# Depthwise taps moved from VectorE to ScalarE and accumulating transfers in one more unit per image

## Chip, cores and metric

The kernel runs on one core of one Trainium2 chip. The metric is the device time of one execution in microseconds (us), the median of several runs. Five engines of the core work side by side, each through its own instructions in a fixed order: TensorE (PE, matrix products), VectorE (DVE), ScalarE (ACT), GpSimd (POOL, here the issuer of accumulating transfers) and SyncE (SP, the issuer of the other transfers). An instruction that needs a result of another engine waits for it, and what stands behind it in the same queue waits too.

## What is computed

The input is 32 images of 96 channels and 56x56 points in fp32. Layer 0 is an inverted bottleneck with a residual. Layer 1 works on the 3136 points of an image as tokens: a frequency mixer and a small feed-forward part with rounded operands, each behind a layer norm and with a residual. Cut to what matters:

```python
h = relu(bn(einsum('oc,bchw->bohw', w1, x)))    # 96 -> 576 channels
h = relu(bn(dwconv3x3(h, wdw)))                 # nine taps for each channel
x = x + bn(einsum('oc,bchw->bohw', w2, h))      # 576 -> 96 channels
t = tokens(x)
t = t + attn(ln(t))     # 96 -> 192, DFT over tokens, scale, relu, inverse DFT, 192 -> 96
t = t + ffn(ln(t))      # 96 -> 384 -> 96 with fp8 products
```

The change concerns the depthwise convolution alone: each of 576 channels is multiplied by nine weights at nine offsets, and the nine products are summed.

## The kernel before

**Units.** An image is cut in two halves of 28 rows (s = 0 and 1). The hidden channels 0 to 511 are four blocks of 128 (k = 0 to 3); one half of one block is a *unit* (`unit`, line 595), eight per image, 256 in all. The last 64 channels go another way: `last_channels` runs their taps on TensorE as products with banded matrices (lines 719 to 784).

**A unit.** TensorE expands 96 channels to 128 (L617) into PSUM, and ScalarE evicts two pieces with bias and relu into the tile `hs` of 29 rows (L627). ScalarE then starts the sum `acc` with one tap and the bias (L643, `begin`). The other taps reach `acc` in one of two ways. As a rule VectorE does a tap as one multiply-add over the whole tile (L670, `tap`). The tap (0,0) always goes the second way: ScalarE writes weight times `hs` into a tile `product` (L659), and a transfer that adds on arrival, issued by GpSimd, adds that tile to `acc` (L678, `add`). In blocks k = 1 and 3 (`DOUBLE`, line 143) a second tap, (-up, 0), is also a ScalarE product; a first transfer adds it to the product of tap (0,0), and a second adds the sum to `acc`. So a unit with one product has seven taps on VectorE and one transfer, and a unit with two has six taps and two transfers. At the end ScalarE applies relu to `acc` in place (L687, `finish`). Here up = 1 - 2s, so that in the second half (-up, 0) is the tap (1, 0), which covers 27 of the 28 rows.

**The rest of an image.** `front` multiplies the finished units with w2 and the residual's identity in PSUM (L883, L902, L920), and ScalarE evicts (L933); a layer norm on VectorE follows. `mixer_in`, `mid` and `back` are products on TensorE with evictions on ScalarE and some VectorE work in between (among them L987 to L1042, L1123 to L1263, L1329 to L1463).

**Buffers.** `hs` has 3 buffers, `acc` 7, `product` 3; PSUM has 3 general tiles (`ps`) and one for `front` (`pw`).

**What sets the order.** No scheduler of the compiler does; the kernel holds a planner (`Plan`). Each piece of work is a step with an engine, an assumed cost, the steps that it waits for, the buffers that it takes and frees, an assumed delay until others see its result, and a rank. The planner walks through time, and whenever an engine is free it emits there the ready step of lowest rank whose buffers are free. The order that comes out is the fixed order of each engine's instructions on the chip. Every image advances the rank by 32 and every unit by 4; `OFF` and `AT` place the parts of a unit around that (product of tap (0,0) at +3.0, second product at +0.5).

**Fillers.** Where the planner finds TensorE idle with work left[...], it puts in a dummy 128x128 product (`filler`, L1491)[...]. A filler is part of the fixed order: on the chip it runs at its place whether TensorE would be idle or not. One filler shows as two records in the profile.

Of the kernel before, what the change touches and what calls it, by code (L numbers as in the profile page):

```python
# [142 lines left out]
DOUBLE = (1, 3)  # L143
# [15 lines left out]
class Plan:  # L159
# [54 lines left out]
    def step(self, engine, cost, emit, after=(), take=(), give=(), late=None, rank=None):  # L214
        late = self.LATE.get(engine, 0.1) if late is None else late
        if rank is None:
            rank = self.now
            self.now += self.pace
        s = Step(engine, cost, emit, list(after), list(take), list(give), late, rank, len(self.steps))
        self.steps.append(s)  # L220
        return s
# [62 lines left out]
def tile_kernel(ctx: ExitStack, tc: tile.TileContext, d: dict, out: bass.AP):  # L284
# [12 lines left out]
    def psum():  # L297
        return psa.tile([128, 2, 512], F32, name="ps", tag="ps")
# [131 lines left out]
    def scale_of(g, v, p, n):  # L430
        s, r, w = tmp(p, n), tmp(p, n), tmp(p, n)
        nc.vector.tensor_scalar_add(v, v, EPS)
        nc.scalar.activation(r, v, AF.Sqrt)
        newton(s, r, v, w)
        nc.vector.tensor_mul(s, s, g)
        return s
# [6 lines left out]
    s = scale_of(vec[:, 0, :], vec[:, 3, :], 128, NK + 1)  # L443
# [14 lines left out]
    s = scale_of(vec[:, 4, :], vec[:, 7, :], 128, NK + 1)  # L458
# [97 lines left out]
    def pe(n, m, passes):  # L556
        return passes * max(0.855 * n, 0.88 * m) / 1000

    def act(n, columns=0, source=0.05):
        return source + 0.835 * n / 1000 + 0.093 * columns  # L560

    def dve(n, fixed=0.13):
        return fixed + n / 960
# [36 lines left out]
    def unit(img, s, k):  # L600
        n = (2 * img + s) * NK + k
        o = R * s - base[s]
        up = 1 - 2 * s
        u = {}

        def weight(dr, dc):
            at = 3 * (dr + 1) + dc + 1
            return wdw[:, k, at : at + 1]

        def expand(h):  # L610
            def mm():
                if h == 0:
                    u["hs"] = w2.tile([128, XR, S], F32, name="hs", bufs=3)
                u[h] = psum()
                for j in range(2):
                    at = (2 * h + j) * QW
                    nc.tensor.matmul(  # L617
                        u[h][:, j, 0:QW],
                        lhsT=w1T[:, 128 * k : 128 * (k + 1)],
                        rhs=xs[img, s][0:C, at : at + QW],  # L620
                        start=True,
                        stop=True,
                    )

            def evict():
                flat = u["hs"].rearrange("p r c -> p (r c)")
                nc.scalar.activation(  # L627
                    flat[:, 2 * h * QW : 2 * (h + 1) * QW].rearrange("p (j w) -> p j w", j=2),
                    u[h][:, :, 0:QW],
                    AF.Relu,  # L630
                    bias=b1[:, k : k + 1],
                )

            after = [loaded[img, s]] if h == 0 else [u["first"]]
            e = u["first"] = step("PE", pe(QW, 128, 4), mm, after, ["ps"] + ["hs"] * (h == 0), rank=4 * n + OFF[0] + h)
            return step("ACT", act(2 * QW, 1), evict, [e], [], ["ps"], rank=4 * n + OFF[0] + h)

        e = [expand(0), expand(1)]

        def begin():  # L640

            acc[img, s, k] = w1.tile([128, R, S], F32, name="acc", bufs=7)
            nc.scalar.activation(  # L643
                acc[img, s, k],
                u["hs"][:, o + up : o + up + R, :],
                AF.Identity,
                scale=weight(up, 0),
                bias=bd[:, k : k + 1],
            )

        def span(dr, dc):

            return max(0, -(o + dr)), min(R, XR - o - dr), max(0, -dc), S - max(0, dc)

        def product(dr):
            def f():
                ra, rb, _, _ = span(dr, 0)
                u["p", dr] = w1.tile([128, R, S], F32, name="product", bufs=3)
                nc.scalar.activation(  # L659
                    u["p", dr][:, ra:rb, :], u["hs"][:, ra + o + dr : rb + o + dr, :], AF.Copy, scale=weight(dr, 0)  # L660
                )

            return f

        def tap(dr, dc):
            def f():
                ra, rb, ca, cb = span(dr, dc)
                src = u["hs"][:, ra + o + dr : rb + o + dr, ca + dc : cb + dc]
                dst = acc[img, s, k][:, ra:rb, ca:cb]
                nc.vector.scalar_tensor_tensor(dst, src, weight(dr, dc), dst, ALU.mult, ALU.add)  # L670

            return f

        def add(to, dr):
            def f():
                ra, rb, _, _ = span(dr, 0)
                t = acc[img, s, k] if to is None else u["p", to]
                nc.gpsimd.dma_start(  # L678
                    out=t[:, ra:rb, :].rearrange("p r c -> p (r c)"),
                    in_=u["p", dr][:, ra:rb, :].rearrange("p r c -> p (r c)"),  # L680
                    accum_op=ALU.add,
                )

            return f

        def finish():
            nc.scalar.activation(acc[img, s, k], acc[img, s, k], AF.Relu)  # L687

        t = step("ACT", act(W, 2, 0.09), begin, e, ["acc"], rank=4 * n + OFF[1])
        c = [step("ACT", act(W, 1, 0.09), product(0), e, ["product"], rank=4 * n + AT[0])]  # L690
        rest = [q for q in TAPS[1:] if q != (up, 0)]
        if k in DOUBLE:

            rest.remove((-up, 0))
            c.append(step("ACT", act(W, 1, 0.09), product(-up), e, ["product"], rank=4 * n + AT[1]))
        for at, q in enumerate(rest):
            last = q == rest[-1]
            t = step("DVE", dve(W - 28, 0.16), tap(*q), [t] + c * last, [], ["hs"] * last, rank=4 * n + OFF[2] + at * 3.5 / len(rest))
        if k in DOUBLE:
            c = [step("POOL", 1.0, add(0, -up), c, [], ["product"], late=(W * 128 * 4, SOFT), rank=4 * n + AT[1])]  # L700
        t = step("POOL", 1.0, add(None, 0), [t] + c, [], ["product"], late=(W * 128 * 4, SOFT), rank=4 * n + 3)
        ready[img, s, k] = step("ACT", act(W, 0, 0.09), finish, [t], rank=4 * n + OFF[3])
# [775 lines left out]
    for i in range(nimg):  # L1478
        for s in range(2):
            load_half(i, s)  # L1480
            last_channels(i, s)
            for k in range(NK):
                unit(i, s, k)
            front(i, s)
        for half in range(2):
            mid(i, half)
        for h in range(4):
            back(i, h)
# [70 lines left out]
```

## Time and profile before

The median of three runs is 4476.41 us (4473.82 to 4477.92). The profiled execution has a span of 4469.5 us.

| engine | busy, us | share of the span | instructions |
|---|---|---|---|
| PE | 4366.5 | 98% | 34916 |
| DVE | 4307.1 | 96% | 7053 |
| ACT | 4103.5 | 92% | 5390 |
| POOL | 339.6 | 8% | 403 |

The granted TensorE clock is 0.994 of full speed on average. The 16 DMA engines move 789.43 MB; the queue of the accumulating transfers (q0, software_dynamic) has 304.64 MB of it and takes 34.2% of the engines' time.

How to read it: a share of busy time is taken over the whole span, with its start (filling the pipeline) and its end (emptying it). In the long middle part the same pattern repeats: the first `acc` transfers of successive images start 134.6 us apart from the fifth image on. What one image costs there, times the images, makes up most of the time. In the view of groups of instructions each row gives a line of the kernel, the engine, the operation, the tiles, the shape, the count, the busy time in all, the mean of one in ns, and the idle time of the engine just before them with what ended it. Durations of neighbours overlap a little on ACT, DVE and PE[...].

### The profile page before, as it was taken

The page shows a single profiled execution, that of the slowest core. Times are in us where ns is not written, and L with a number is a line of the kernel's source. Part 1 is how long each engine was busy: PE and PEld are TensorE (multiplying, and loading weights), DVE is VectorE, ACT ScalarE, POOL GpSimd, SP SyncE. Part 2 cuts the span into 40 slices and gives each one's busy share as a digit, 9 for nine tenths or more (in the row PEclk, how much of TensorE's full clock was granted, in tenths as well). Part 3 has the DMA queues.
Part 4 walks back from the last instruction along what each step waited for, and adds up shares of the span by engine and source line. Part 5 has one row for each costly group of instructions (what it writes and reads, how often), then busy time and mean ns, then how long its engine had stood idle before and what let it go on. Part 6 is the DMA issues. An engine that isn't in the chain of part 4 may idle for free.

```text
span 4469.5 us, 87997 instructions
## 1 busy us (share of the span) xinstructions
PE 4366.5 (98%) x34916; PEld 3248.3 (73%) x34916; DVE 4307.1 (96%) x7053; ACT 4103.5 (92%) x5390; POOL 339.6 (8%) x403
## 2 busy tenths in 40 slices
PE   8999999999999999999999999999999999999998
PEld 5767777777777777777777777777777777777777
DVE  8999999999999999999999999999999999999977
ACT  5778999999999999999999999999999999999975
POOL 1100000000000000000000000000000000000000
PEclk9999999999999999999999999999999999999999
DMA  5667777777777777777777777777777777777763
GB/s 106 144 147 174 192 172 184 189 176 183 192 171 188 187 176 184 189 176 184 187 173 191 187 174 188 182 176 192 184 176 188 176 180 194 180 177 191 169 180 107
DMA packets 390992, 789.43 MB, mean 177 GB/s; under 512 B 135696, under 2 KB 236628, under 8 KB 390580
## 3 DMA queue, kind: packets, MB, share of 16 engines
q1 hardware_dynamic: 335028, 479.15, 38.1%
q0 software_dynamic: 55488, 304.64, 34.2%
q8 instruction: 275, 4.51, 0.4%
q14 instruction: 137, 1.12, 0.1%
q10 hardware_dynamic: 64, 0.01, 0.0%
HBM read 286.38 MB, written 192.68 MB: 107 GB/s over the span
## 4 chain that ended last, share of the span: by engine, by line
PE 37%; DVE 32%; ACT 15%; issue 3%; DMA 3%; ACTq 0%; DVEq 0%; POOLq 0%; SPq 0%
DVE acc L670 20%; PE pw L883 10%; PE ps L617 5%; PE ps L1005 3%; PE ps L1036 3%; PE ps L1123 3%; PE ps L1329 2%; ACT h L1395 2%; DVE sb L1152 2%; DVE V L1152 2%; DMA acc<-product 2%; ACT product L659 1%; ACT hs L627 1%; PE ps L755 1%; PE ps L1447 1%
## 5 line engine op out<-in xcount | busy, mean ns | idle before, releaser
L670 DVE SCALAR_TENSOR_TENSOR acc<-hs,wdw,acc 128x1540 f32<-128x1540 f32 (+2 forms) x1664 | 2970.5, 1795 | 5.9 <-ACT acc L643 0.3
L617 PE MATMUL ps<-xs,w1T 96*128 96x406 f32 x2048 | 808.9, 517 | 27.2 <-ACT al L784 12.9
L883 PE MATMUL pw<-w2T,acc 128*112 128x96 f32 x7168 | 788.6, 264 | 3.8 <-ACT acc L687 3.7
L883 PEld LDWEIGHTS pw<-w2T,acc 128*112 128x112 f32 x7168 | 750.5, 179 | 57.5 <-issue 34.6
L659 ACT ACTIVATE product<-hs,wdw 128x1568 f32<-128x1568 f32 (+1 forms) x384 | 610.8, 1599 | 15.2 <-DMA product<-product 15.0
L617 PEld LDWEIGHTS ps<-xs,w1T 96*128 96x128 f32 x2048 | 355.6, 190 | 291.5 <-issue 165.1
L627 ACT ACTIVATE hs<-ps,b 128x812 f32<-128x812 f32 x512 | 481.3, 940 | 84.4 <-PE ps L617 79.5
L678 POOL DMA_DIRECT2D acc<-product x256 | 223.3, 872 | 3709.6 <-DVE df L855 687.2
L643 ACT ACTIVATE acc<-hs,bd,wdw 128x1568 f32<-128x1568 f32 x256 | 436.9, 1707 | 0.2
L755 PE MATMUL ps<-hl,band 128*64 128x385 f32 (+3 forms) x3072 | 418.7, 497 | 4.8 <-ACT hs L627 4.8
L687 ACT ACTIVATE acc<-acc 128x1568 f32<-128x1568 f32 x256 | 388.0, 1516 | 26.1 <-DMA acc<-product 19.9
L1005 PEld LDWEIGHTS ps<-watt,xnT 97*120 97x120 f32 x1792 | 293.2, 182 | 97.3 <-issue 40.8
L1005 PE MATMUL ps<-watt,xnT 97*120 97x192 f32 x1792 | 339.1, 330 | 19.8 <-DVE V L1152 14.7
L1123 PEld LDWEIGHTS ps<-wb,yb 112*128 112x128 f32 x3528 | 297.0, 164 | 48.1 <-issue 35.8
L1410 ACT ACTIVATE h<-h 128x784 fp8e5<-128x784 f16 x348 | 300.2, 863 | 34.4 <-DVE h L1401 34.3
L1395 ACT ACTIVATE h<-ps 128x784 f16<-128x784 f32 x384 | 317.0, 828 | 12.3 <-PE ps L1383 11.5
L1350 ACT ACTIVATE u<-tt,mf,rf 112x96 fp8e5<-112x96 f32 x812 | 317.0, 465 | 0.7
L1123 PE MATMUL ps<-wb,yb 112*128 112x112 f32 x3528 | 317.2, 269 | 0.0
L755 PEld LDWEIGHTS ps<-hl,band 128*64 128x64 f32 (+1 forms) x3072 | 152.7, 135 | 203.0 <-issue 163.4
L1401 DVE TENSOR_SCALAR h<-h,b1q 128x784 f16<-128x784 f16 x384 | 162.3, 423 | 88.9 <-ACT h L1395 88.8
L1036 PE MATMUL ps<-z,wa 56*64 56x384 f32 (+1 forms) x2048 | 223.9, 498 | 1.7 <-ACT hs L627 1.7
L1329 PE MATMUL ps<-gd,wd 114*112 114x96 f32 x1792 | 200.2, 264 | 2.3 <-DMA gd<-gdr 2.0
(171 smaller groups left out, 6621.3 us busy)
## 6 DMA issues: line engine op xcount, KB each, us to landing
acc<-product POOLq DMA_DIRECT2D x256, 784.0 KB, 8.7
product<-product POOLq DMA_DIRECT2D x128, 756.0 KB, 11.2
yb<-ydr SPq DMA_DIRECT2D x252, 294.0 KB
wd<-in_wd_dram SPq DMA_DIRECT2D x128, 349.1 KB
wb<-in_wb_dram SPq DMA_DIRECT2D x63, 686.0 KB
ydr<-ya SPq DMA_DIRECT2D x256, 168.0 KB
xs<-in_x_dram SPq DMA_DIRECT2D x64, 609.0 KB
tdr<-xt SPq DMA_DIRECT2D x64, 588.0 KB
```

The source lines that it names most:

```text
L617: nc.tensor.matmul(u[h][:, j, 0:QW], lhsT=w1T[:, 128 * k : 128 * (k + 1)], rhs=xs[img, s][0:C, at : at + QW], start=True, stop=True,)
L627: nc.scalar.activation(flat[:, 2 * h * QW : 2 * (h + 1) * QW].rearrange("p (j w) -> p j w", j=2), u[h][:, :, 0:QW], AF.Relu, bias=b1[:, k ...
L643: nc.scalar.activation(acc[img, s, k], u["hs"][:, o + up : o + up + R, :], AF.Identity, scale=weight(up, 0), bias=bd[:, k : k + 1],)
L659: nc.scalar.activation(u["p", dr][:, ra:rb, :], u["hs"][:, ra + o + dr : rb + o + dr, :], AF.Copy, scale=weight(dr, 0))
L670: nc.vector.scalar_tensor_tensor(dst, src, weight(dr, dc), dst, ALU.mult, ALU.add)
L687: nc.scalar.activation(acc[img, s, k], acc[img, s, k], AF.Relu)
L755: nc.tensor.matmul(pv[:, :, ca:cb], lhsT=band[rows, j, dc + 1, 64 * o : 64 * o + 64], rhs=H[rows, q : q + 7, ca + dc : cb + dc], skip_grou ...
L883: nc.tensor.matmul(u["pw"][0:SK, t, n % 4, 0:C], lhsT=src[rows, (G * t + n) * SK : (G * t + n + 1) * SK], rhs=rhs, skip_group_check=True, **k,
L1005: nc.tensor.matmul(pv[0:PK, q - a, 0:HA], lhsT=xnT[:, q, 0:PK], rhs=watt, start=True, stop=True,)
L1036: nc.tensor.matmul(u["y", b][64 * c : 64 * c + n, j, 0 : 2 * HA], lhsT=wa[at, 0:n], rhs=rhs, start=True, stop=True)
L1123: nc.tensor.matmul(o, lhsT=lhsT, rhs=u["wb"][:, G * s + q, :], start=True, stop=True)
L1395: nc.scalar.activation(u["h", c].rearrange("p (j w) -> p j w", j=2), u["H", c][:, :, 0:n], AF.Copy)
```

## The change

One more unit per image, the first block of the second half (k = 0, s = 1), sends two taps through ScalarE and the accumulating transfers. It is meant to take work off VectorE and give it to ScalarE, whose share of busy time is lower, and to the transfers. Nothing else is edited; ranks, buffers and the planner's constants stay. Since all orders come from the planner, the orders of all engines are made anew.

```diff
         rest = [q for q in TAPS[1:] if q != (up, 0)]
-        if k in DOUBLE:
+        double = k in DOUBLE or (k == 0 and s == 1)
+        if double:
 
             rest.remove((-up, 0))
             c.append(step("ACT", act(W, 1, 0.09), product(-up), e, ["product"], rank=4 * n + AT[1]))
         for at, q in enumerate(rest):
             last = q == rest[-1]
             t = step("DVE", dve(W - 28, 0.16), tap(*q), [t] + c * last, [], ["hs"] * last, rank=4 * n + OFF[2] + at * 3.5 / len(rest))
-        if k in DOUBLE:
+        if double:
             c = [step("POOL", 1.0, add(0, -up), c, [], ["product"], late=(W * 128 * 4, SOFT), rank=4 * n + AT[1])]
         t = step("POOL", 1.0, add(None, 0), [t] + c, [], ["product"], late=(W * 128 * 4, SOFT), rank=4 * n + 3)
```

## The prediction

> **What bounds the kernel now.** I read the busy time in stretches first, since start and end differ from the middle: 0 to 400 us fills the pipeline, 800 to 4000 us repeats one image, the rest empties it. The columns are stretch, length, then busy us and instructions of PE, PEld, DVE, ACT and POOL, the TensorE clock, the DMA share and GB/s.
>
> ```profile
> 0.00:400.00 400.00, 363.03 (x2628) 264.36 (x2628) 366.15 (x431) 273.42 (x282) 39.25 (x58) 0.96 0.64 142
> ...
> 800.00:4000.00 3200.00, 3164.86 (x25406) 2337.00 (x25408) 3143.53 (x5093) 3076.81 (x4089) 247.17 (x285) 1.00 0.75 183
> 4000.00:4470.00 470.00, 447.67 (x3755) 353.47 (x3751) 406.38 (x898) 375.16 (x520) 21.94 (x25) 0.99 0.63 161
> ```
>
> In the middle PE is busy 98.9%, DVE 98.2%, ACT 96.1%. An image takes 134.6 us there (from one image's first `acc` transfer to the next one's), so per image PE is idle 1.5 us, DVE 2.4, ACT 5.2. Only in the first 400 us is ACT far below DVE (273 against 366).
>
> Three engines so near to full need a second look: who waits for whom. These are the waits of 800 to 4000 us, first of DVE, then ACT, then PE (total us, times, longest).
>
> ```profile
> DVE h L1401 <- ACT h L1395: 50.7, 71, 1.2
> ```
>
> ```profile
> ACT al L784 <- PE ps L755: 43.8, 47, 1.0
> ACT hs L627 <- PE ps L617: 39.1, 49, 1.2
> ACT h L1410 <- DVE h L1401: 29.9, 46, 0.9
> ACT acc L687 <- DMA acc<-product: 0.3, 1, 0.3
> ```
>
> ```profile
> PE ps L1005 <- DVE V L1152: 11.2, 23, 0.5
> PE ps L617 <- ACT al L784: 10.8, 47, 0.2
> PE ps L617 <- ACT h L1395: 7.7, 25, 0.4
> ```
>
> DVE waits almost only for ACT (2.1 us per image: 50.7 x 134.6/3200), never for an `acc`, a `product` or a lack of taps. ACT waits mostly for PE (82.9 us of its waits, 3.5 per image). PE waits little for anybody (29.7 us, 1.25 per image). The lag starts at PE and travels to ACT and then to DVE. The chain of waits of one image (2053 to 2188 us) says the same in legs: about 50 us on PE (one leg without a break from 2053 to 2094), 57 on DVE, 19 on ACT. In the PE leg stand fillers (start us, us, what):
>
> ```profile
> 2055.52 0.35 PE ps L1362 x7
> 2055.87 0.73 PE pw L1491 x6
> 2056.60 2.09 PE ps L1036 x8
> 2058.69 0.44 PE ps L1383 x2
> 2059.13 0.22 PE pw L1491 x2
> ```
>
> The planner put them where it thought TensorE idle; on the chip TensorE runs behind by then, and they lie on the chain that sets the pace.
>
> [...] So 98.9% may hide slack, and I looked at starts instead of ends: taking for every PE group the distance to the next start near its shortest (tenth percentile over 1000 to 3040 us), the groups fill 95.3% of the time, DVE's 97.4%, ACT's 94.3%. [...] PE has up to 3.6% more than its idle time[...]. [...] Here the clock is 1.00 through the middle; how much of that the fillers do, no run here shows. [...] all 384 such transfers are on q0.
>
> **The change, part by part** (per image, in the middle). The groups that give the prices:
>
> ```profile
> L659 ACT ACTIVATE product<-hs,wdw 128x1512 f32<-128x1512 f32 x128 | 200.2, 1564 | 0.1
> ```
>
> ```profile
> L670 DVE SCALAR_TENSOR_TENSOR acc<-hs,wdw,acc 128x1512 f32<-128x1512 f32 x128 | 228.5, 1785 | 1.1
> ```
>
> - DVE loses one tap of 128x1512. Its row says 1.785 us, but starts of neighbours lie 1.70 us apart: **-1.70**. In all 32 x 1.70 = 54 us, the most that VectorE can give back.
> - ACT gains one product of 128x1512: row 1.564, start to start 1.45: **+1.45** (46 us in all). It fits in ACT's 5.2 us of idle time, but that time is waits for PE, in pieces of up to 1.2 us.
> - POOL gains one issue (0.86 us busy per issue); POOL is 8% busy: nothing, hidden behind its own idle time.
> - The transfer: 756 KB more on q0. q0 uses 34.2% of 16 engines for 384 transfers, so 0.09% each; 32 more make 2.9%, on a DMA share of 75%: bandwidth is no bound. Landing has a median of 11.2 us for `product` and 8.7 for `acc`; a unit with two products needs both in turn.
> - New waits: the unit's last tap on DVE now also waits for the second product, which is ranked 2.5 earlier than the first and so is done. Its `finish` on ACT waits for two landings; behind it in ACT's queue are evictions that free PSUM for PE. The middle shows 0.3 us of such a wait in 24 images. From below it costs 0, from above 1 us per image (the 0.3 to 3.9 us that single such waits took elsewhere, some of the time); I take 0.
> - The `product` ring of 3 now serves three units with two products in a row (k = 3 of half 0, k = 0 and 1 of half 1). ACT waited five times for it, 15.0 us in all, none in the middle. I take 0, at most 1 us.
> - PE: its work is the same, but the order is not. The order in which the built programs' instructions stand has 585 fillers before and 723 after: per image 8 before; 13 after from the tenth image on. In the images before that the count differs by -2 to +10. Of the five new ones one stands in the long PE leg, four in the other half after L1036, where PE runs without a recorded gap before (2000 to 2035 us). Three fillers take 0.82 us start to start, so 0.27 each: 5 x 0.27 = **+1.35**.
>
> The sum for the likeliest case, with PE as the pace: +1.35 for the fillers; against it stands what DVE's relief takes from PE's waits, at most the wait for L1152, 11.2 x 134.6/3200 = 0.47. So about +0.9 per image over the last 23 images, +20 us. In images 4 to 8 fillers hardly differ: 0. In the first four, where DVE is ahead of ACT, most of 4 x 1.70 = 6.8 us is gained: -5. The tail has no taps after 4270 us: 0. Together +15: **4491 us**.
>
> **Rivals.**
> - *VectorE is the bound after all.* For it: 97.4% by starts, the highest of the three; the unit's taps (near 2042 to 2058 us) lie on a DVE leg of the chain; PE may absorb fillers in gaps that its modelled ends hide. Against it: DVE waits for ACT, ACT for PE. With all of the tap passed on, 4476 - 54 = 4422; with two thirds, **4440**. This is the other side.
> - *Nothing moves.* Fillers fall into waits that PE has anyway and DVE's relief only lengthens DVE's waits: **4476**. For it: loads per image that trade 1.70, 1.45 and 1.35 against each other.
> - *ScalarE comes late.* Its 1.45 us, or a wait for a `product` buffer or a landing, delays evictions that PE waits for. For it: ACT's idle time is in small pieces, and the ring is tighter. Against it: ACT fills only 94.3% by starts. About 1 us per image more than the likeliest case, 28 images: **4520**.
>
> **How the numbers follow.** Likeliest 0.40 (0.02 of it within 0.2%), VectorE 0.36, nothing 0.12, ScalarE 0.12. Slower 0.38 + 0.12 = 0.50, same 0.02 + 0.12 = 0.14, faster 0.36. The range leaves out the lower part of the VectorE case (about 0.12) and the upper part of the last (0.06): 4436 to 4522.
>
> **What would show it.** If right, the image period is 135 to 136 us, PE stays at 99% with about 34 us more L1491 than before in 800 to 4000 us (some 21 of its images have the five more: 21 x 5 x 2 records x 0.16 us), DVE falls to 96 or 97% and its waits for L1395 grow, and waits of L687 and L659 for transfers stay near zero. If VectorE was the bound, the period is near 133.5 us, DVE stays at 98%, and PE's busy share grows although it has more fillers. If ScalarE comes late, L659 or L687 show waits for transfers, or PE waits for ACT grow past 2 us per image. The prediction is wrong at its root if fillers cost nothing, that is if PE's groups lie closer together after than before.

## Result and profile after

The changed kernel takes 4580.13 us (median, 4569.13 to 4591.22), the kernel before 4475.73 us beside it. The ratio is 1.0233, 95% interval 1.0207 to 1.0259: 104 us slower, where 15 us slower was forecast and 4522 us was the upper end of the range. Lines below L689 stand one line further down in the changed kernel (L1401 is now L1402). The edits of the experiments shift lines again; the engine and the tile tell which one is meant: the finish, `ACT acc` waiting for `acc<-product`, is L687 here and L698 where the planner's code has grown above it.

The busy time of the middle, with the columns as before (PE, PEld, DVE, ACT, POOL, clock, DMA share, GB/s):

```profile
800.00:4000.00 3200.00, 3119.82 (x24869) 2330.27 (x24868) 3035.59 (x4906) 3020.74 (x3985) 264.97 (x300) 0.99 0.76 183
```

All three big engines do less per microsecond: PE fell from 98.9 to 97.5%, DVE from 98.2 to 94.9%, ACT from 96.1 to 94.4%. None of them is the new bound; something makes them all wait. An image takes 138.9 us (mean of 20 images, first `acc` transfer to first), 4.2 more than the 134.7 of before. The waits of 800 to 4000 us name it; DVE, then ACT, then PE (total us, times, longest):

```profile
DVE eo L1168 <- ACT V L1159: 53.3, 21, 3.4
DVE acc L670 <- ACT acc L643: 26.9, 25, 1.2
...
DVE h L1402 <- ACT h L1396: 16.2, 48, 0.9
```

```profile
ACT acc L687 <- DMA acc<-product: 65.6, 23, 3.9
ACT hs L627 <- PE ps L617: 40.0, 67, 1.0
ACT al L785 <- PE ps L756: 20.1, 23, 1.3
```

```profile
PE ps L1124 <- ACT hs L627: 48.8, 21, 3.2
```

Before, the finish L687 waited 0.3 us for a landing in this stretch. Now it waits 65.6 us, once per image and 2.9 us each time, and the largest waits of PE and DVE in total are for ScalarE instructions. One such place, first in ScalarE's timeline (start us, us, instruction, idle before it), then in TensorE's:

```profile
2042.32 0.85 ACT L1019 ACTIVATE z<-ps 120x768 f32<-120x768 f32 x1
2046.88 1.51 ACT L687 ACTIVATE acc<-acc 128x1568 f32<-128x1568 f32 x1 [3.70 <-DMA acc<-product]
2048.29 0.92 ACT L627 ACTIVATE hs<-ps,b 128x812 f32<-128x812 f32 x1
2049.11 0.85 ACT L1159 ACTIVATE V<-V 128x784 f32<-128x784 f32 x1
```

```profile
2045.81 0.50 PE L1384 MATMUL ps<-uT,w1q 96*128 96x392 fp8e5 x2
2049.27 3.33 PE L1124 MATMUL ps<-wb,yb 112*128 112x112 f32 x14 [2.95 <-ACT hs L627]
2052.38 2.97 PE L884 MATMUL pw<-w2T,acc 128*112 128x96 f32 x16
```

The finish stands at the head of ScalarE's queue for 3.7 us. Behind it stand the eviction L627, which TensorE needs to get a PSUM tile back, and L1159, which VectorE needs. ScalarE stops first, at 2043.2 us. TensorE has work until 2046.3 and VectorE until 2046.8; then both wait for what stands behind the finish, 2.95 and 3.17 us. VectorE's line:

```profile
2049.99 0.63 DVE L1168 SCALAR_TENSOR_TENSOR eo<-sb,m2rb,V 128x392 f32<-128x392 f32 x1 [3.17 <-ACT V L1159]
```

After that the two TensorE groups take about twice as long as elsewhere (3.33 instead of 1.71 us, 2.97 instead of 1.72). The chain of waits through the same place (start us, us, what) leads to one transfer:

```profile
2033.52 1.83 DVE acc L670
...
2035.96 10.89 DMA acc<-product
2046.85 0.02 issue
2046.88 0.03 ACT acc L687
2046.90 1.39 issue
2048.29 0.93 ACT hs L627
```

The transfer was issued right after the unit's last tap and landed 10.9 us later. The planner's constants give it 1.0 us, its bytes at 225 GB/s (3.6 us) and `SOFT` = 1.3 us, 5.9 in all when nothing else moves. Pairing issues and finishes in order shows whose finish it is: the first of each image's eight, the unit k = 0, s = 0, which the change doesn't touch (60.6 us of waiting from image 9 to 29; no other unit above 1.1). In the kernel before, that unit's finish starts 10.0 us after the issue too (median; 10.2 now), but other instructions keep ScalarE busy until then. The new order offers it some 3 us earlier. The landing itself is less than 1 us later (median of this unit's landings 9.4 us after the issue before, 10.1 now, images 9 to 29).

The granted TensorE clock falls there too, as the stretches of the same place show (the clock stands after POOL's column):

```profile
2040.00:2045.00 5.00, 5.00 (x32) 3.98 (x31) 4.96 (x13) 3.17 (x6) 0.00 (x0) 1.00 1.06 227
2045.00:2050.00 5.00, 2.05 (x11) 1.58 (x11) 1.83 (x3) 3.12 (x4) 0.00 (x0) 0.82 0.91 209
2050.00:2055.00 5.00, 5.00 (x28) 5.00 (x26) 5.00 (x7) 5.00 (x7) 0.00 (x0) 0.50 0.39 100
2055.00:2060.00 5.00, 5.00 (x50) 3.52 (x50) 3.98 (x8) 3.47 (x6) 0.86 (x1) 1.00 1.09 255
```

In stretches of a quarter of a microsecond the clock is 1.00 up to 2048.00 us, 0.84 in the next, and 0.50 from 2048.25 to 2055.00 us. Here it fell 1.7 to 1.9 us after the end of TensorE's last product (2045.81 + 0.50). Adding up, over stretches of 5 us from 400 to 4440 us, the length times the share of the clock that wasn't granted, 56 us of clock time are lost in the changed kernel, 8 before. Three causes offer themselves: the late landing, the fillers (the prediction's), and the dips of the clock. And behind them the question whether the work or the order is at fault.

### The profile page after: what moved, and what is told of

The parts are those of the page before. It is cut to its first block, busy times and chain, and to the rows that moved or that the text cites. A ratio compares the mean times of both kernels' runs of the same rounds, so it can differ in the third digit from the quotient of the medians.

```text
span 4589.3 us, 88627 instructions
## 1 busy us (share of the span) xinstructions
PE 4433.6 (97%) x35192; PEld 3329.8 (73%) x35192; DVE 4283.9 (93%) x7021; ACT 4155.6 (91%) x5422; POOL 372.7 (8%) x435
## 4 chain that ended last, share of the span: by engine, by line
PE 56%; ACT 15%; DVE 14%; DMA 9%; issue 5%; SPq 1%; POOLq 0%; ACTq 0%; DVEq 0%
PE pw L884 12%; PE ps L617 10%; DVE acc L670 9%; DMA acc<-product 7%; PE ps L1124 5%; PE ps L756 4%; PE ps L1037 3%; PE ps L1006 2%; PE ps L1330 2%; PE ps L1429 2%; PE ps L720 2%; ACT product L659 2%; ACT acc L643 2%; PE ps L1222 2%; PE ps L1384 2%
## 5 line engine op out<-in xcount | busy, mean ns | idle before, releaser
L670 DVE SCALAR_TENSOR_TENSOR acc<-hs,wdw,acc 128x1540 f32<-128x1540 f32 (+2 forms) x1632 | 2924.8, 1798 | 43.7 <-ACT acc L643 34.3
L884 PEld LDWEIGHTS pw<-w2T,acc 128*112 128x112 f32 x7168 | 777.4, 183 | 59.9 <-issue 39.1
L884 PE MATMUL pw<-w2T,acc 128*112 128x96 f32 x7168 | 814.9, 269 | 4.1 <-ACT acc L687 4.1
L659 ACT ACTIVATE product<-hs,wdw 128x1568 f32<-128x1568 f32 (+1 forms) x416 | 660.0, 1595 | 12.1 <-DMA product<-product 11.7
L627 ACT ACTIVATE hs<-ps,b 128x812 f32<-128x812 f32 x512 | 480.8, 940 | 81.1 <-PE ps L617 77.4
L617 PEld LDWEIGHTS ps<-xs,w1T 96*128 96x128 f32 x2048 | 367.5, 191 | 241.7 <-issue 183.3
L687 ACT ACTIVATE acc<-acc 128x1568 f32<-128x1568 f32 x256 | 387.7, 1514 | 95.2 <-DMA acc<-product 89.5
L643 ACT ACTIVATE acc<-hs,bd,wdw 128x1568 f32<-128x1568 f32 x256 | 435.8, 1702 | 0.4
L1124 PEld LDWEIGHTS ps<-wb,yb 112*128 112x128 f32 x3528 | 312.5, 170 | 111.8 <-ACT hs L627 62.2
L1124 PE MATMUL ps<-wb,yb 112*128 112x112 f32 x3528 | 337.3, 277 | 57.6 <-ACT hs L627 53.0
L1037 PE MATMUL ps<-z,wa 56*56 56x384 f32 (+1 forms) x2048 | 242.6, 504 | 9.7 <-ACT o L1464 3.5
L1492 PE MATMUL pw<-ident 128*128 128x128 f32 x1446 | 216.6, 286 | 2.0 <-ACT xt L934 2.0
L1492 PEld LDWEIGHTS pw<-ident 128*128 128x128 f32 x1446 | 195.8, 197 | 29.9 <-issue 21.8
## 6 DMA issues: line engine op xcount, KB each, us to landing
product<-product POOLq DMA_DIRECT2D x160, 756.0 KB, 10.7
```

The source lines that it names most:

```text
L617: nc.tensor.matmul(u[h][:, j, 0:QW], lhsT=w1T[:, 128 * k : 128 * (k + 1)], rhs=xs[img, s][0:C, at : at + QW], start=True, stop=True,)
L627: nc.scalar.activation(flat[:, 2 * h * QW : 2 * (h + 1) * QW].rearrange("p (j w) -> p j w", j=2), u[h][:, :, 0:QW], AF.Relu, bias=b1[:, k ...
L643: nc.scalar.activation(acc[img, s, k], u["hs"][:, o + up : o + up + R, :], AF.Identity, scale=weight(up, 0), bias=bd[:, k : k + 1],)
L659: nc.scalar.activation(u["p", dr][:, ra:rb, :], u["hs"][:, ra + o + dr : rb + o + dr, :], AF.Copy, scale=weight(dr, 0))
L884: nc.tensor.matmul(u["pw"][0:SK, t, n % 4, 0:C], lhsT=src[rows, (G * t + n) * SK : (G * t + n + 1) * SK], rhs=rhs, skip_group_check=True, **k,
L1037: nc.tensor.matmul(u["y", b][64 * c : 64 * c + n, j, 0 : 2 * HA], lhsT=wa[at, 0:n], rhs=rhs, start=True, stop=True)
```

## Experiments

Ratios are to the kernel before on the same chip, with 95% intervals.

**The late landing: the finish emitted later.** The planner plans as before; only the emission of this one step is held until five more ScalarE steps have been emitted (edit cut to what matters).

```diff
-                    s.emit()
+                    if s.hold:              # 5 for finish of k == 0, s == 0
+                        held.append([s.hold, s.emit])
+                    else:
+                        s.emit()
+                        # after each ACT step: count down, emit what is due
```

> The changed kernel with one instruction moved: in each image the relu in place (finish, L687) of the unit k = 0, s = 0 is emitted five ACT steps later; all other orders, the work and the fillers stay. Theory 'late landing': ACT waits at this finish for the acc transfer (65.6 us in 800 to 4000 us, 23 times, 2.9 us each), everything behind it in ACT's queue is late, TensorE starves and its clock falls to half. Then about 30 x 2.9 = 87 us of waiting go, and with them the clock dips: 4490 us or less (4470 to 4500), waits of L687 below 15 us, clock 0.99 or more. Theory 'fillers' (the prediction's: +1.35 us per image of TensorE time): little changes, above 4550 us. Theory 'work' (one more product on ACT and one more transfer cost the time): above 4550 us.

Measured: 4504.03 us, ratio 1.0073 (1.0058 to 1.0089). ScalarE's waits in the middle:

```profile
ACT hs L638 <- PE ps L628: 48.5, 89, 1.0
ACT al L798 <- PE ps L769: 20.2, 23, 1.3
ACT acc L698 <- DMA acc<-product: 12.5, 19, 1.6
```

One instruction moved per image takes back 1.6% (1.0233 to 1.0073, some 72 us). The wait shrinks from 65.6 to 12.5 us, PE no longer shows the wait of L1124, 3 us of clock time are lost instead of 56, and an image takes 135.6 us. What is left of the wait is the next unit's finish (k = 1, s = 0). The time is 4 us above what was expected of this cause and 46 below what the other two ask for: the late landing is shown to be the larger part of the loss. The rest, 33 us, is nearly all in the middle, at about 1 us per image.

**The same, eight steps later.**

> As e5 (4504 us), but the finish of the unit k = 0, s = 0 is emitted eight ACT steps later instead of five. In e5 the finish of the next unit waits for its landing (10.8 us in 20 images), that of the first no more. If what is left over the kernel before (30 us) were the same wait, 4490 to 4497; if it is the ScalarE work (d12: +19 us over d1) and the order of TensorE, 4500 to 4510.

Measured: 4509.12 us, 1.0080 (1.0063 to 1.0097), with 13.4 us of waiting left. No further gain; the rest isn't the landing of this unit. The next unit's wait stayed, so that one remains untried.

**The fillers left out,** in the changed kernel, in the one with the finish moved, and in the kernel before:

```diff
-                    self.filler()
+                    if not 700 < now < 4100:
+                        self.filler()
```

> The changed kernel with the planned fillers left out between 700 and 4100 us of the planner's time; the order of all else stays. Theory 'fillers': 314 fillers less at 0.27 us give 85 us back, about 4495 us. Theory 'late landing': fillers are beside the point; TensorE waits instead, and its clock may fall more often: 4570 to 4620 us, waits of L687 as before at 2.9 us per image.

> The finish moved later as in e5 (4504 us), and the fillers of the middle left out too. With the late landing out of the way TensorE should set the pace again, as the prediction had it. If its step on fillers is right (0.27 us each, on the path), 314 fillers less give up to 85 us: 4420 to 4470. If fillers lie in TensorE's waiting even then: 4495 to 4510, or more if the clock falls.

> The kernel before without its fillers between 700 and 4100 us of the planner's time, 200 fillers less; the rest of the order stays. Theory of the prediction (a filler in a leg of TensorE costs 0.27 us on the path): 200 x 0.27 = 54 us less, 4420, two thirds 4440. If fillers lie in waiting that is there anyway (e3, g2): 4470 to 4480. If they hold the clock up: above 4490, clock below 0.99.

Measured: 4586.41 us, 1.0253 (1.0232 to 1.0274); 4511.11 us, 1.0081 (1.0065 to 1.0098); 4465.93 us, 0.9990 (0.9983 to 0.9997). Leaving out 314 fillers doesn't help either of the first two (the second lies 1 us above what was expected of fillers in waiting); leaving 200 out of the kernel before saves 5 us, 0.025 us each instead of 0.27, and leaves the granted clock where it was (0.994 to 0.997, in its runs as in those of the kernel before). The PE waits of the kernel before without fillers say where their time was:

```profile
PE ps L1037 <- ACT o L1464: 13.0, 26, 0.5
PE ps L1006 <- DVE V L1153: 11.4, 24, 0.5
```

With them out, L1037 (the group behind them) waits for a ScalarE eviction; that wait wasn't in the list before. The fillers had filled it, as the planner meant them to. Of the 54 us, 13 are in this wait and 5 were gained; where the other 36 went, the list of waits doesn't show. The time is 4 us below the 4470 to 4480 expected of fillers that lie in waiting, so they cost a little, not nothing.

**Fillers against the dips.** Ten fillers more per image, just ahead of the L1124 group that starves:

```diff
                 u["X", part] = psum()
+                if part == 1 and half == 0 and 5 < img < 31:
+                    for _ in range(10):
+                        filler()
```

> The changed kernel with ten fillers more per image (images 6 to 30) just where TensorE starves behind the late finish (before the L1124 group that waits 2.3 us for an eviction L627). It keeps TensorE active through the wait. If the clock dips (58 us of lost clock in the changed kernel after 400 us, 8.6 before, by windows of 5 us) cost time on the path, it gets faster by 10 to 45 us in spite of 2.7 us more TensorE work per image, and the clock goes back to 0.99; the waits of L687 stay. If the dips lie off the path or the fillers cost more than they save, it gets slower by up to 25 x 2.7 = 68 us. The theory 'fillers' says slower by 68 us.

Measured: 4595.53 us, 1.0277 (1.0261 to 1.0293). The timeline of TensorE at the starving group:

```profile
2043.36 2.39 PE L1495 MATMUL pw<-ident 128*128 128x128 f32 x20
2045.69 1.81 PE L1127 MATMUL ps<-wb,yb 112*128 112x112 f32 x14
2047.34 1.72 PE L884 MATMUL pw<-w2T,acc 128*112 128x96 f32 x16
```

The fillers fit into the wait, and both groups run at full clock (1.00 in the stretches 2040 to 2045 and 2045 to 2050 us), about 2.8 us faster than in the changed kernel; lost clock time falls from 56 to 19 us. Yet the kernel doesn't get faster (0.4% slower than the changed kernel). TensorE's waits in the middle show where part of the time went:

```profile
PE ps L1432 <- ACT ya L1043: 17.4, 20, 0.9
PE ps L617 <- DVE V L1156: 16.0, 21, 0.8
```

In the changed kernel these two waits were 4.4 and 0.3 us. So TensorE, faster through the two groups, waits further on for some half of what it gained. No cost of the dips on their own shows here; that the additional fillers cost some microseconds which hide a small gain, the run can't exclude.

**Order or work: the new order with the old work.** The second product of the unit and its transfer emit nothing, and VectorE does that tap right after another of the unit:

```diff
+            c.append(step("ACT", ..., (lambda: None) if new else product(-up), ...))
+            c = [step("POOL", 1.0, (lambda: None) if new else add(0, -up), ...)]
+    # taps(q): tap(*q), and tap(-up, 0) after tap(-up, -1) where new
```

> The order that the planner made for the changed kernel, with the work of the kernel before: the second product of the unit k = 0, s = 1 and its transfer are left out where they stand, and VectorE does that tap beside another of the same unit. Theory 'order' (the loss lies in where instructions stand): still slow, 4560 us or more, with the waits of the finish for its landing. Theory 'work': back near 4476 us, since ACT has 1.45 us and the transfers 756 KB less per image.

Measured: 4598.20 us, 1.0278 (1.0261 to 1.0295). The wait is there too:

```profile
ACT acc L687 <- DMA acc<-product: 85.5, 42, 6.2
```

From image 9 to 29 the unit k = 0, s = 0 waits 64.1 us, as in the changed kernel (60.6), though there is no additional transfer: the late landing comes with the order. Another 16.6 us are waits of the unit k = 1, s = 1 (1.1 in the changed kernel), just behind the unit in which VectorE has its tap back. So the run shows that the order loses the time without the new work; that it loses more so is in part a late landing of its own.

With the finish five steps later as well:

> e2 (the order made for the changed kernel, the work of the kernel before, 4598 us) with the finish of the unit k = 0, s = 0 emitted five ACT steps later, as in e5. e5 stands at 4504 with the changed work. If the 30 us by which e5 is above the kernel before are ScalarE's additional product (d12 - d1 = 19 us) and the transfer: 4475 to 4490. If they are the new order itself: 4495 to 4515. If old work in this order meets other late landings: above 4520.

Measured: 4527.40 us, 1.0119 (1.0104 to 1.0134), with waits for landings left, from image 9 to 29 11.8 us at the unit k = 1, s = 0 as with the new work (10.8), and 12.8 again at k = 1, s = 1 (1.2):

```profile
ACT acc L698 <- DMA acc<-product: 30.3, 36, 4.5
```

In this order the new work is faster by about 0.46% than the old, with the late finish (1.0233 against 1.0278) and without it (1.0073 against 1.0119). How much of that is the new work and how much those waits isn't separated.

**The old order with the new work, in parts.** In the kernel before, the tap is left out where it stands; then also the product is made beside the first (the edits in words). Both kernels lack that tap's term in their sums; they only price the work.

```diff
+    tap step of (-up, 0) with k == 0 and s == 1: emits nothing          # both
+    product step of k == 0 and s == 1: product(-up)(), then product(0)()  # second
```

> The kernel before, its order untouched, with one VectorE tap per image left out (tap (1,0) of the unit k = 0, s = 1; that term is missing from the sum). It prices the relief alone. Theory 'TensorE sets the pace': 0 to 0.47 us per image, so 4461 to 4476 beside 4476. Theory 'VectorE is the bound': 32 x 1.70 = 54 us less, 4422; two thirds, 4440.

> The kernel before, its order untouched but for one instruction: the tap is left out as in d1, and ScalarE makes the second product of that unit beside the first; no transfer adds it (that term is missing from the sum). It is the engines' work of the change without the new order and without the transfer. If the change of work is harmless: as d1, within 10 us. If 1.45 us more on ScalarE is passed on: 32 x 1.45 = 46 us above d1.

Measured: 4471.77 us, 0.9997 (0.9989 to 1.0006), and 4491.16 us, 1.0041 (1.0026 to 1.0056). In that order VectorE's relief is worth nothing, and ScalarE's product costs 0.44%, some 20 us of the 46 it takes, between the two expectations. Half of it is lost in the first six images (752.6 against 742.3 us); in the middle an image takes 135.1 us instead of 134.7. Where the 1.70 us went shows in DVE's waits of the first of the two, beside those of before (50.7 us for L1395 and nothing for L643):

```profile
DVE h L1401 <- ACT h L1395: 57.4, 94, 1.2
DVE acc L670 <- ACT acc L643: 27.8, 24, 1.2
```

VectorE got to the next unit earlier and waited there for its start on ScalarE. The additional transfer in the old order wasn't tried, and so neither was the whole of the new work there.

**The change turned round.** In the old order the unit k = 1, s = 1 gives up its second product and transfer, and VectorE does the tap.

> The kernel before, its order untouched, with the change turned round: the unit k = 1, s = 1 gives up its second product and transfer, and VectorE does that tap beside another (32 x 1.70 = 54 us more VectorE, 32 x 1.45 = 46 us less ScalarE). If VectorE's slack is what d1 suggests only one way, and VectorE is nearly full: 4480 to 4520. If ScalarE's work is the dearer one (d12): 4455 to 4470.

Measured: 4517.14 us, 1.0097 (1.0082 to 1.0112), +43 us by the ratio of VectorE's 54, though ScalarE has 46 us less to do. PE now waits for VectorE at a new place, and longer at an old one (11.2 us before, at L1152):

```profile
PE ps L617 <- DVE tt L1344: 29.2, 23, 1.3
PE ps L1015 <- DVE V L1162: 18.5, 23, 0.9
```

So in the old order more VectorE work is nearly all paid for, and less isn't rewarded. In this order more work on VectorE and more on ScalarE both cost time, and what VectorE is spared it spends waiting; no single engine is shown to be the bound.

**The planner told the landing.** `SOFT` from 1.3 to 4.3 us in the changed kernel, and in the kernel before as the control:

```diff
-SOFT = 1.3
+SOFT = 4.3
```

> The changed kernel with the planner's constant for what an adding transfer takes beyond its bytes (SOFT) at 4.3 instead of 1.3 us, so that a landing is planned at 1.0 + 3.6 + 4.3 = 8.9 us after the issue, near the 8.2 to 10.7 us of the medians. Theory 'late landing': the planner puts the finish where its landing is, waits of L687 fall below 15 us in 800 to 4000 us, and the time to 4460 to 4510. If the order is bad for another reason: above 4550.

> The kernel before, with the planner's constant SOFT at 4.3 instead of 1.3 us as in e6, and no other edit: the same work in an order that is made anew. It is the control for e6 (4567 us). Theory 'any new order costs' (the order of before fits the chip, and one made under other assumptions does not): 4510 to 4600, though no finish waits. Theory 'the new unit makes the order bad': 4460 to 4490, so that e6 lies above it by 80 us or more.

Measured: 4566.62 us, 1.0209 (1.0194 to 1.0224), and 4586.37 us, 1.0252 (1.0237 to 1.0267). In the first that wait falls to 1.0 us in the middle, as expected, but the time is nearly as slow as the changed kernel's and not the expected 4460 to 4510: the order lost its time in other places. The control is what matters: with the old work and nothing changed but a constant of the planner, the kernel loses as much as by the change. No finish waits for a landing in its middle. Of the two it is the one without the new work that is slower, by 0.4%, though their orders differ. The largest waits of ScalarE are many and small, and for TensorE:

```profile
ACT hs L627 <- PE ps L617: 46.3, 116, 0.7
ACT al L784 <- PE ps L755: 32.9, 35, 1.3
ACT pj L1235 <- PE ps L1221: 30.1, 34, 1.4
ACT V L1135 <- PE ps L1123: 28.7, 23, 1.9
ACT h L1395 <- PE ps L1383: 28.7, 34, 1.4
```

**Small steps of the same constant,** 1.5 and 1.1 us, in the kernel before:

> The kernel before with SOFT at 1.5 instead of 1.3 us, the same work in an order made anew (3403 of 5394 places of ACT's order hold another kind of instruction). Control for e7 with a small step. If any order but that of before costs time: 4500 to 4600. If e7 was slow because its constant is far off: 4460 to 4485.

> The kernel before with SOFT at 1.1 instead of 1.3 us, the same work in an order made anew (1447 of 5394 places of ACT's order differ). As h2, on the other side: 4500 to 4600 if any new order costs time, with waits of some finish (L687) for its landing if the landing is the usual way of losing it; 4460 to 4485 if not.

Measured: 4503.61 us, 1.0070 (1.0055 to 1.0085), and 4535.48 us, 1.0139 (1.0122 to 1.0156). The first loses in the start and at the end: its first six images take 22 us more than before (the fourth 144.3 us, before 137.9), and what follows the last image's first `acc` transfer 7 us more. Its middle is nearly as before (134.9 us per image, before 134.7). The second has late landings again: L687 waits 24.6 us in 36 times. All three orders made anew for the same work are slower, by 0.7 to 2.5%; in the middle two of them are, and one hardly.

## Why the prediction was wrong

The direction was right, by luck: it came from the fillers, which cost next to nothing. The size (15 us for 104) and the cause were not right.

- **The step that failed first: "New waits ... I take 0"** for the finish behind its landing. The prediction looked for that wait at the new unit with its two landings. It came at another unit, one that the edit doesn't touch, because all orders were made anew. It measured 2.9 us per image, over the bound of 1 us set from above, and moving that one instruction took back 72 us. The bound was read from the waits of the old order, and these didn't show where the new one would put this finish. The mechanism was in the rival "ScalarE comes late", with 4520 us too small and the unit wrong.
- **Fillers, +1.35 us per image: wrong.** The count was right (34 us more busy time of fillers in the middle, as worked out), the price was not: 0.27 us is what a filler takes, 0.025 us is what it cost. That they stood on the chain of waits was no proof that they set the pace: without them TensorE waits for ScalarE behind them, 13 us in the middle. Fillers that cost nothing were the prediction's own sign of being wrong at its root.
- **"PE sets the pace": too simple.** VectorE's relief was worth nothing, as argued (0.9997). But more VectorE work cost 43 of 54 us and more ScalarE work 20 of 46. The waits that led from PE to ACT to DVE were no proof that PE was full; here each engine waited a little for another.
- **ScalarE's product "fits in ACT's 5.2 us of idle time": wrong** in the old order, by 0.6 us per image on the mean and 0.4 in the middle (135.1 against 134.7). That idle time was not all reserve.
- **Right:** the `product` ring (11.7 us of waits in all, none in the middle) and the transfers' bandwidth (DMA share 0.75 to 0.76; landing medians 8.2 and 10.7 us, before 8.7 and 11.2).

What the change does to the time is then: an order that loses 1.6% by one late landing, and 0.7% that remains with the finish moved. That remainder isn't settled. The old work in the same order, finish moved, isn't faster (1.0119). It has 18 us more of landing waits in the middle (30.3 against 12.5); with these taken off, an estimate, it is still 0.8% above the kernel before. So this order seems to lose as much with the old work, but how order and new work share the remainder isn't shown. That orders made anew lose 0.7 to 2.5% with the old work is shown for three of them, one of them mostly outside the middle; why the order of before is better than all of these is open. That less VectorE work and more ScalarE work might pay in an order that fits it isn't excluded by these runs.

## What to carry to other kernels

Where a planner or scheduler makes the order, an edit changes two things, the work and the order. Split them: keep the order and empty or fill single steps, and keep the work and make the order anew by a harmless change of a constant. If the harmless change costs as much as the edit, the edit hasn't been judged yet. A price taken from the old trace needs proof in the new order: the wait near zero became 2.9 us per image here, and the filler on the chain of waits cost a tenth of its time even in the old order. A long transfer's landing is a good first place to look, since what stands behind the instruction that waits for it waits too (here 10.9 us from issue to landing, 3.7 us of waiting at the finish, and 2.95 us of TensorE behind it).

## What was not expected of the hardware

- A TensorE clock granted at half (0.50 from 2048.25 to 2055.00 us at the place shown; 56 us of clock time lost in all) had no cost of its own that the runs show: with 37 us of it taken back by fillers put into TensorE's waiting, the time didn't fall (1.0277 against 1.0233).
- Two hundred dummy matrix products of 0.27 us, taken from a TensorE that is 98.9% busy by the profile, gave back 5 us of their 54, and without them the granted clock did not fall (0.994 to 0.997 with them and without).
